# The end of a selective-scan block: six slots and a hand-ordered tail become one written list

## The chip, the cores and the metric

The kernel runs on one core of a Trainium2 chip. The metric is device microseconds of one execution, from start to end, and the time of a kernel is the median of several executions. Beside the times there is one profiled execution with a record of every instruction; its time and its span (first to last instruction) are told apart below. The core's engines run side by side, each in the order in which its instructions were written: TensorE (PE, with weight loads as PEld), VectorE (DVE), ScalarE (ACT), GpSimd (POOL) and SyncE (SP), which here only issues transfers.

## What is computed

For x of shape 4 x 128 x 96 x 96 the block adds to x a mixture of four scans of the normalised image (rows and columns, forward and backward). Cut to its core:

```
def _scan1d(x, ...):
    t = _grouped1x1(x, in_proj_w, in_proj_b, G)
    u, gate = t[:, :HID], t[:, HID:]
    u = depthwise_conv5(silu(u))
    s = _conv1x1(u, ssm_in_w)
    a = DMIN + (DMAX - DMIN) * sigmoid(_conv1x1(u, ssm_delta_w, ssm_delta_b))
    bb, cc = tanh(_conv1x1(u, ssm_b_w, ssm_b_b)), tanh(_conv1x1(u, ssm_c_w, ssm_c_b))
    h[l] = a[l] * h[l-1] + bb[l] * s[l]
    u = u + _conv1x1(cc * h + ssm_d * s, ssm_out_w)
    u = _grouped1x1(u * sigmoid(gate), mix_w, mix_b, G)
    return _conv1x1(u, out_proj_w, out_proj_b)
y = concat(scan of rows, rows reversed, columns, columns reversed)
x = x + einsum(fuse_w, y) + fuse_b
```

The reference writes the recurrence of h with cumulated logarithms; the line above is what it amounts to.

## The kernel before

Four images, for each a column pass (V) and a row pass (H), each pass six steps, each step four residues p in the order 1, 0, 3, 2: that makes NPAIR = 192 **pairs**, numbered n. A pair is two scans at once (s = 0 forward, s = 1 backward) over 384 positions. mix_w, out_proj_w and fuse_w are multiplied into one matrix w_fin beforehand, so a pair's last product goes straight to the 128 output channels and is added to `acc`, which holds the image's x in SBUF. The steps of the second half of a pass meet the positions of the first half again, so their silu values and gates come back from DRAM (`load_silu`, `load_kept`, `load_last`) and need no in-projection.

The work on a pair is cut into short **operations**, written by `emit` (L965). With engine, line and what each does:

- PE, L184: C0 C1 (convolution by bands), L (its rest, where p is not an edge), P1a P0a P1b P0b (projections to a, b, c, s), W00 W01 W10 W11 (result, s then half j). PE, L810: S00 S01 S10 S11 (state into the hidden channels).
- DVE: T1 to T4 (taps, L731), E (edge tap, L712, in place of L where p is 0 or 3), SCAN0 SCAN1 (L789, the two halves of a step's recurrence, once per four pairs), GAT0 GAT1 (times gate, L863).
- ACT: T0 (L729), UC (L694), TM (L747), SC (L755), CT (L758), SS (L776), UND0 UND1 (L806, copies u under the state), YS0 YS1 (L874, L876, takes the result out of its bank).
- POOL: DEC (L769), BS (L772), CH (L795), ADD (L799), CP (L803, copies the state's input to the other 64 partitions; on ACT for the last six pairs), ACC0 ACC1 (L910, adds the result to acc).

Within a pair the order of need is: C, L, T0 to T4; P; TM, SC, CT; DEC, BS; SCAN over four pairs; CH, ADD, CP; UND and S into the same banks; GAT; W; YS; ACC; and, for the second half of a row pass, the transfer of finished stretches of acc to `out` (`send`, L880).

**Order.** The engines run under a manual schedule: the order of writing is the order on each engine. `slot(t)` (L998) writes slot t by one of four texts in PLAN, picked by t modulo 24 (slots 186 and 187 use "none", 188 to 191 "front"). Each operation has a lag: slot t holds C of pair t, W of pair t - 7, and so on. After slot 191, `tail` (L1046) writes what is left by hand: for each of the last pairs S, then W of the pair before, GAT, UND of the next, CH ADD CP of the one after, and `finish` (L1036), which adds s = 0 on POOL from YS0 and s = 1 on DVE straight from the bank.

**Banks.** PSUM has eight banks, and twelve would be wanted: taps, convolution and the two UND/S/GAT groups take two each, P1a/P0a/TM, P1b/P0b/SC/CT and the two W groups one each. `rent` hands a bank to the first operation of a group, by the text's wish if that bank is free, else the one given back longest ago; `give` returns it after the group's last operation. A PE operation whose bank was read by DVE or ACT before waits for that reading.

**Loads.** SP issues in order. `load_edge` (L705) fills a tile with one buffer; `load_kept` fills one of two gate tiles for pair n + 2 after GAT of pair n; `load_last` brings the last four pairs' gates into a silu tile, after slot 189. A step's four transfers of 384 KB to `out` go after the step's last pair.

Of the kernel before, what the change touches and what calls it, by code (L numbers as in the profile page):

```python
# [47 lines left out]
P = 128  # L48
# [70 lines left out]
}  # L119
TBUFS, YBUFS, SEEDS = 6, 1, ()  # L120
ORDER = (1, 0, 3, 2)
# [4 lines left out]
def conv_preact_kernel(  # L126
# [769 lines left out]

    def accumulate(n, s, adder=nc.gpsimd):
        un = units[2 * n + s]
        p, st, y = un["p"], un["st"], yss.pop((n, s))
        if s == 1:  # L900
# [9 lines left out]
        adder.tensor_add(part, y, part)  # L910
        if un["order"] == "H" and un["st"] >= NS // 2 and un["k"] == R - 1:
            done[s].extend((un["b"], bass.ts(2 * st + e, LN * WW // 2)) for e in range(2))
# [68 lines left out]
    def release(kind):  # L981
        while held and loaded[pair_of(held[0][1])["b"]] == 2 * NS:
            emit(*held.pop(0), kind)

# [13 lines left out]
    def slot(t):  # L998
        now[0] = t
        kind = slot_kind(t)  # L1000
        for op in PLAN[kind].split():
            n = t - LAGS.get(op, 0)
            if op == "PIECE":
                if later and later[1] and t % R != 1:
                    free[:] = rent("tiny", kind)
                    later[1] = next(later[0], None)
# [12 lines left out]
            else:  # L1019
                if op == "YS0":  # L1020
                    load_next()
                if op[:2] == "YS":
                    if sum(h[0][3] == op[2] for h in held) == 2 - int(op[2]):
                        release(kind)
                emit(op, n, kind)
# [9 lines left out]

    def finish(n):  # L1036

        accumulate(n, 0)
        b = where.pop(("W1b", n))[0]
        yss[n, 1] = bank(b)[:, :N]  # L1040
        accumulate(n, 1, nc.vector)
        give([b])
        send(0)
        send(1)

    def tail():  # L1046

        def run(n, ops):
            for op in ops.split():
                if op == "DECV":  # L1050
                    decay(n, nc.vector)
                else:
                    emit(op, n, "none")

        last = NPAIR - 1
        run(last - 4, "CH")
        run(last, "P1b P0b")
        run(last - 7, "YS1")
        run(last - 6, "W00 W01 W10 W11")
        run(last - 4, "ADD")  # L1060
        run(last, "TM SC CT DECV BS")
        run(last - 5, "CP UND0 UND1 S00 S01 S10 S11")
        run(last - 3, "SCAN0 SCAN1")
        run(last - 7, "ACC1")
        run(last - 5, "GAT0 GAT1")
        run(last - 4, "CP")
        run(last, "SS")
        run(last - 1, "SS")
        run(last - 6, "YS0 YS1 ACC0")
        run(last - 4, "UND0 UND1")  # L1070
        run(last - 5, "W00 W01 W10 W11")
        run(last - 4, "S00 S01 S10 S11")
        run(last - 3, "CH ADD CP")
        run(last - 6, "ACC1")
        run(last - 5, "YS0")
        finish(last - 5)
        run(last - 4, "GAT0 GAT1")
        run(last - 3, "UND0 UND1")
        run(last - 2, "CH ADD CP")
        for n in range(last - 3, last + 1):  # L1080
            run(n, "S00 S01 S10 S11")
            run(n - 1, "W00 W01 W10 W11 YS0")
            run(n, "GAT0 GAT1")
            if n < last:
                run(n + 1, "UND0 UND1")
            if n + 2 <= last:
                run(n + 2, "CH ADD CP")
            finish(n - 1)
        run(last, "W00 W01 W10 W11 YS0")
        finish(last)  # L1090

# [24 lines left out]
    for op in PLAN["front"].split():  # L1116
        for n in range(-LAGS.get(op, 0)):
            if op[0] != "F" and op[:3] != "SIL":
                emit(op, n, "front")
    with tc.manual_schedule(  # L1120
# [3 lines left out]
    ):  # L1124
        for t in range(NPAIR):
            slot(t)
# [79 lines left out]
```

## Time and profile before

| what | us |
|---|---|
| median of 3 runs | 1815.69 (1810.68 to 1819.12) |
| profiled execution, its own time | 1816.33 |
| profiled execution, its span | 1814.6 |
| PE busy in it | 1761.8 (97%) |
| DVE busy | 1516.6 (84%) |
| ACT busy | 1492.9 (82%) |
| POOL busy | 1410.5 (78%) |

The profile's page gives busy time by engine, the span in 40 slices (a digit is a tenth), the granted TensorE clock, the chain of waits that ended last, and groups of instructions. The trace behind it can be asked for an engine's instructions in order of time (start, length, engine, line, operation, output <- input, shape, count, and in brackets the idle time before and what ended it), for busy times by stretches, and for transfers. PE rows count an f32 matmul twice, so C0 and C1 together, eight matmuls, are x16. A PE row's length includes the emptying of the array, so pitches are taken from start to start. The end of the program is where the core does worst: the last two of PE's 40 slices are the only ones below 9 after the second.

### The profile page before, as it was taken

What the parts mean: (1) busy time and instruction counts of PE and PEld (TensorE: products, weight loads), DVE (VectorE), ACT (ScalarE), POOL (GpSimd) and SP (SyncE); (2) the same over time, 40 slices, a digit from 0 to 9 for tenths busy, and PEclk for the clock granted to TensorE, in tenths of its full rate; (3) what the DMA queues carried; (4) which work ended last, traced back from release to release, by engine and by line L of the source; (5) the groups of instructions that cost most, each with busy time, mean ns of one, the idle gap of its engine ahead of it and who ended that gap; (6) DMA issues with size and microseconds to landing.
All of it is one profiled execution on the core that took longest, in us unless ns stands there. A gap on an engine that the chain in (4) does not pass through costs nothing.

```text
span 1814.6 us, 54530 instructions
## 1 busy us (share of the span) xinstructions
PE 1761.8 (97%) x22560; PEld 638.5 (35%) x22560; DVE 1516.6 (84%) x1538; ACT 1492.9 (82%) x2582; POOL 1410.5 (78%) x1504
## 2 busy tenths in 40 slices
PE   6899999999999999999999999999999999999987
PEld 3233333333333333333333333333333333333332
DVE  4788988888789988988888898888888888788874
ACT  4788888888888888888888888888888888888864
POOL 4478888778778888787777888877777888877884
PEclk7999999999999999999999999999999999999998
DMA  8467676665987578555897667656598765756452
GB/s 249 132 206 239 190 228 178 201 210 168 285 264 248 196 223 238 174 195 155 245 284 236 219 199 235 187 190 210 167 276 250 247 207 152 216 163 208 164 211 82
DMA packets 182568, 377.70 MB, mean 208 GB/s; under 512 B 16688, under 2 KB 145840, under 8 KB 182320
## 3 DMA queue, kind: packets, MB, share of 16 engines
q1 hardware_dynamic: 181888, 373.24, 66.2%
q8 instruction: 178, 2.92, 0.7%
q10 hardware_dynamic: 432, 0.96, 0.1%
q14 instruction: 70, 0.57, 0.1%
HBM read 222.96 MB, written 151.18 MB: 206 GB/s over the span
## 4 chain that ended last, share of the span: by engine, by line
PE 85%; DMA 4%; DVE 3%; ACT 3%; issue 2%; SPq 1%; POOL 1%; POOLq 0%; DVEq 0%; ACTq 0%
PE psum L184 72%; PE psum L810 9%; PE psum L816 4%; DMA acc<-in_xr 2%; DVE psum L731 1%; DMA out<-acc 1%; DMA edge<-edge 1%; ACT gate L822 1%; DVE u L863 1%; ACT psum L806 0%; POOL acc L910 0%; DVE u L731 0%; SPq L659 0%; ACT psum L729 0%; POOL t L772 0%
## 5 line engine op out<-in xcount | busy, mean ns | idle before, releaser
L731 DVE SCALAR_TENSOR_TENSOR psum<-sil,small,psum 128x768 f32<-128x768 f32 x576 | 588.6, 1022 | 55.2 <-ACT psum L729 37.0
L184 PE MATMUL psum<-u,w_fin 128*32 128x384 f32 x6144 | 585.9, 494 | 6.3 <-DVE u L863 3.0
L910 POOL TENSOR_TENSOR acc<-ys,acc 128x384 f32<-128x384 f32 x378 | 441.3, 1176 | 177.8 <-ACT ys L874 85.1
L184 PE MATMUL psum<-u,main 128*32 128x384 f32 x6144 | 563.9, 489 | 8.6 <-DVE u L712 3.3
L863 DVE SCALAR_TENSOR_TENSOR u<-gate,psum 128x768 f32<-128x768 f32 x376 | 345.8, 951 | 109.3 <-PE psum L810 81.0
L184 PEld LDWEIGHTS psum<-u,main 128*32 128x32 f32 x6144 | 185.5, 110 | 331.3 <-issue 213.8
L806 ACT COPY psum<-u 128x768 f32<-128x768 f32 x352 | 277.7, 801 | 29.4 <-DVE u L731 12.6
L184 PEld LDWEIGHTS psum<-u,w_fin 128*32 128x32 f32 x6144 | 176.0, 110 | 352.4 <-issue 247.0
L184 PE MATMUL psum<-sil,band 128*32 128x384 f32 x3072 | 284.9, 487 | 7.1 <-DVE u L731 2.7
L795 POOL TENSOR_TENSOR t<-t,t 64x384 f32<-64x384 f32 x192 | 235.0, 1224 | 62.2 <-DVE t L789 28.3
L810 PE MATMUL psum<-t,main 32*128 32x384 f32 x1536 | 263.6, 532 | 6.1 <-ACT psum L806 6.1
L799 POOL TENSOR_TENSOR t<-t,t 64x384 f32<-64x384 f32 x192 | 237.5, 1237 | 7.8
L822 ACT ACTIVATE gate<-psum,bnorm 128x384 f32<-128x384 f32 x384 | 212.4, 577 | 37.0 <-PE psum L810 16.4
L772 POOL TENSOR_TENSOR t<-t,tm 64x384 f32<-64x384 f32 x192 | 197.5, 1029 | 54.8 <-ACT t L755 46.7
L769 POOL TENSOR_SCALAR t<-tm 64x384 f32<-64x384 f32 x191 | 180.8, 947 | 74.5 <-ACT tm L747 35.8
L593 ACT ACTIVATE sil<-psum,bnorm 128x385 f32<-128x385 f32 x384 | 199.9, 582 | 26.8 <-PE psum L184 23.6
L731 DVE SCALAR_TENSOR_TENSOR u<-sil,small,psum 128x768 f32<-128x768 f32 x192 | 194.7, 1014 | 19.2 <-DVE psum L731 1.4
L729 ACT ACTIVATE psum<-sil,small 128x768 f32<-128x768 f32 x192 | 173.8, 905 | 33.4 <-DVE u L863 26.2
L816 PE MATMUL psum<-x_in,wn 32*128 32x384 f32 x768 | 188.5, 516 | 0.4 <-ACT gate L822 0.4
L747 ACT ACTIVATE tm<-psum,small 128x384 f32<-128x384 f32 x192 | 112.4, 585 | 66.9 <-PE psum L184 64.8
L184 PEld LDWEIGHTS psum<-sil,band 128*32 128x32 f32 x3072 | 97.4, 110 | 162.3 <-issue 104.6
L876 ACT COPY ys<-psum 128x384 f32<-128x384 f32 x282 | 135.1, 479 | 23.1 <-POOL acc L910 12.2
(83 smaller groups left out, 1440.7 us busy)
## 6 DMA issues: line engine op xcount, KB each, us to landing
sil<-sil SPq DMA_DIRECT2D x128, 770.0 KB, 6.8
kept<-gate SPq DMA_DIRECT2D x80, 768.0 KB, 4.5
gate<-kept SPq DMA_DIRECT2D x76, 768.0 KB, 6.1
edge<-edge SPq DMA_DIRECT2D x96, 384.0 KB, 6.6
x_in<-in_xs SPq DMA_DIRECT2D x192, 96.2 KB, 3.6
edge<-sil SPq DMA_DIRECT2D x96, 192.5 KB, 3.6
out<-acc SPq DMA_DIRECT2D x48, 384.0 KB, 3.7
acc<-in_xr SPq DMA_DIRECT2D x38, 384.0 KB, 8.4
```

What stands on the lines that cost most here:

```text
L184: nc.tensor.matmul(o[r, : rhs.shape[-1]], lhsT, rhs, start=start, stop=stop, skip_group_check=True)
L593: nc.scalar.activation(sils[step][:, s, j, g, :], bank(frm)[:, : N + 1], AF.Silu, bias=bn[:, 1:2] if j else bn[:, 4 + g : 5 + g],)
L731: nc.vector.scalar_tensor_tensor(u_of(n)[:, :, 1, :] if k == K - 1 else part, src, w_tap[:, k : k + 1], part, ALU.mult, ALU.add,)
L772: nc.gpsimd.tensor_mul(scan_of(n)[0:64, pair_of(n)["p"], :], tbs[n][0:64, :], tms[n][0:64, :])
L795: nc.gpsimd.tensor_mul(ta[0:64, p, :], tbs[n][64:P, :], ta[64:P, p, :])
L799: nc.gpsimd.tensor_add(z, scans[n // R][0:64, pair_of(n)["p"], :], z)
L806: nc.scalar.copy(two(to), us[n][:, s])
L810: nc.tensor.matmul(bank(to)[:, :N], w_so[r, bass.ts(j, P)], tbs[n][r, :], start=not seeded(n), stop=True, skip_group_check=True)
L816: nc.tensor.matmul(bank(to)[:, :N], stats[pair_of(n)["b"]][0][r, s, :], x_in[s][r, q, off : off + N], start=True, stop=True)
L822: nc.scalar.activation(gates[n % 2][:, s, j, :], bank(frm)[:, :N], AF.Tanh, bias=bn[:, 2 + j : 3 + j], scale=0.5,)
L863: nc.vector.scalar_tensor_tensor(v, g, 1.0, two(frm), ALU.add, ALU.mult)
L910: adder.tensor_add(part, y, part)
```

## The change

Slots 186 to 191 and the tail are dropped. In their place stands END, one list of operations for everything that is left, read from left to right: `T1:-6=2` is T1 of pair 192 - 6 = 186, and =2 is the bank wished for if it is the first operation of its group. Operations that do not apply (E of a pair that is no edge) are passed over, as `emit` did before.

Four operations with a star take another engine: CP* runs on ACT, DEC* on DVE, and ACC0*, ACC1* add on DVE straight from the bank (`add_bank`); the YS of the same pair is then left out, and for s = 0 the bias b_fin is added in the same instruction. 16 of the 27 adds in the list have the star, 3 of 7 DEC, 5 of 12 CP.

For the last four pairs (`final`) the sum of result and acc goes into the buffers x_in, idle by then, and each residue's 128 x 384 part is sent at once, two transfers of 192 KB per pair, in place of four of 384 KB behind the last pair. They lie in `out` in another order, which the host turns round by layout alone. `send` follows each ACC; `load_edge` follows an E, `load_kept` the second GAT of a pair, and `load_last` the last reader of the silu tile of pairs up to 187.

```diff
--- before.py
+++ after.py
@@ -117,6 +117,43 @@
+END = """
+    YS1:-14=3 C1:-6 TM:-7=7 CP*:-12 C0:-6=0 W00:-13 T1:-6=2 W01:-13=2 T2:-6 P0b:-7=0 P1b:-7=3
+    UND1:-12 E:-6 UND0:-12=1 ACC1:-14 T3:-6 S10:-12=4 T4:-6 S00:-12 YS0:-13=0 SC:-7 DEC:-7
+    S11:-12=5 S01:-12=0 GAT0:-12=2 T0:-5=5 W11:-13 ACC0:-13 T1:-5=2 W10:-13=0 CH:-11 BS:-7
+    ACC1*:-13 ADD:-11 C0:-5=6 CT:-7=6 GAT1:-12=6 P0a:-6=7 C1:-5 CH:-10 UND0:-11=0 CP:-11 T2:-5=7
+    P1a:-6=1 TM:-6=4 L:-5 W00:-12 CH:-9 T3:-5 P0b:-6=7 ADD:-9 W01:-12=5 S00:-11=6 UC:-5
+    UND1:-11=4 DEC:-6 T4:-5=6 S01:-11=7 ACC0*:-12 S11:-11 T0:-4=5 GAT0:-11 S10:-11=4 SS:-8
+    P0a:-5 P1a:-5=1 W11:-12=7 P1b:-6=4 W10:-12=7 TM:-5=1 T1:-4=3 P1b:-5=6 SC:-6 CT:-6=6 YS1:-12
+    ADD:-10 T2:-4 P0b:-5=2 T3:-4=2 C0:-4 W00:-11=6 SC:-5=5 GAT1:-11=6 DEC:-5 BS:-6 T4:-4=6
+    UND1:-10 BS:-5 W01:-11=3 C1:-4 YS1:-13=6 ACC1:-12 CP:-9 CP*:-10 SCAN0:-8 UND0:-10 S01:-10=2
+    S00:-10=3 S11:-10=0 S10:-10=2 L:-4=6 YS0:-11=7 ACC0:-11 CT:-5 W11:-11=2 GAT0:-10 T0:-3=7
+    GAT1:-10 W10:-11=5 W01:-10 UC:-4=2 W11:-10=1 W00:-10=6 W10:-10=2 T1:-3=5 T2:-3 T3:-3=1
+    ACC0*:-10 YS1:-11 ACC1:-11 YS1:-10=0 C0:-3=4 C1:-3=4 SS:-6 P1a:-4=4 P0a:-4 UND1:-9=1 SS:-7
+    P0b:-4 S11:-9=0 S10:-9 T4:-3=5 UND0:-9=6 ACC1:-10 SCAN1:-8 S01:-9=5 TM:-4 S00:-9=7 E:-3=1
+    P1b:-4=1 CH:-5 T0:-2 GAT1:-9 P1a:-3=3 CH:-8 P0a:-3 C1:-2=5 SS:-5 TM:-3=1 ADD:-8 C0:-2
+    GAT0:-9 T1:-2 UND0:-8 P1b:-3=5 E:-2 CP:-8 SC:-4=4 T2:-2=5 P0b:-3 CT:-4 W00:-9=2 W01:-9=5
+    T3:-2=5 UND1:-8=4 S01:-8 S10:-8 T4:-2=5 CT:-3=6 YS0:-9=7 BS:-4 YS0:-12=7 S00:-8=5 SC:-3=7
+    S11:-8=1 ADD:-5 ACC0:-9 DEC:-4 T0:-1=3 W10:-9 GAT1:-8 W11:-9=0 P1a:-2=1 P0a:-2 C1:-1
+    GAT0:-8=5 P0b:-2=0 C0:-1=6 T1:-1=5 P1b:-2 T2:-1 CH:-7 ADD:-7 W01:-8=4 W00:-8=1 YS1:-9=4
+    ACC1:-9 TM:-2=3 BS:-3 UND0:-7=6 SC:-2=4 T3:-1 L:-1 CP:-7 CH:-6 CT:-2=3 T4:-1=2 SS:-4 ADD:-6
+    P1a:-1=1 UND1:-7=0 S01:-7 S10:-7 S11:-7=7 ACC0*:-8 CP:-6 DEC*:-2 UC:-1=3 S00:-7 SS:-3
+    P0b:-1=4 DEC*:-3 YS0:-8 GAT1:-7=3 P0a:-1=7 UND0:-6=1 UND1:-6=4 P1b:-1=4 TM:-1=2 BS:-2
+    S10:-6=4 GAT0:-7=4 S11:-6 S01:-6 SC:-1=2 CP*:-5 S00:-6 W10:-8=5 CT:-1=4 W11:-8=2 BS:-1
+    UND1:-5=6 YS1:-8 W00:-7 ACC1:-8 DEC*:-1 GAT0:-6 UND0:-5=7 W01:-7=0 W01:-6 SCAN0:-4 W00:-6=5
+    YS0:-7=2 S10:-5 ACC0:-7 SS:-1 SS:-2 SCAN1:-4 CH:-4 S11:-5=3 GAT1:-6=3 S00:-5=5 S01:-5=2
+    ADD:-4 W11:-7 CH:-3 W10:-7=3 GAT0:-5 W10:-6=5 YS1:-7=5 CH:-2 UND1:-4=2 ACC0*:-6 W11:-6=7
+    ADD:-3 W01:-5=6 YS0:-6 YS0:-10 CP:-3 UND0:-4=1 GAT1:-5 W00:-5=6 CP*:-4 S00:-4 ACC1*:-6
+    S01:-4 ACC0*:-5 UND1:-3=7 S10:-4 ADD:-2 GAT0:-4 S11:-4=4 W11:-5=2 YS0:-5 GAT1:-4=5 W10:-5=4
+    W01:-4=3 UND0:-3=1 W00:-4=2 ACC1*:-5 CH:-1 CP*:-2 YS0:-4=0 S11:-3=5 S00:-3=0 ACC0*:-4
+    S01:-3=0 S10:-3=1 GAT0:-3=6 W10:-4=1 W11:-4=1 GAT1:-3 W01:-3 W00:-3=4 UND0:-2=4 UND1:-2
+    ACC1*:-4 ACC0*:-3 S11:-2 ADD:-1 S01:-2=5 S00:-2=1 UND0:-1 ACC1:-7 S10:-2=5 GAT0:-2=3
+    W11:-3=7 CP:-1 W10:-3=2 UND1:-1 GAT1:-2=2 W00:-2=6 S11:-1=3 ACC1*:-3 S01:-1 S00:-1=3 S10:-1
+    YS1:-6 YS1:-4=0 W01:-2=5 YS0:-3=1 YS1:-3 W10:-2 W11:-2 GAT0:-1=2 W00:-1 ACC0*:-2 W01:-1=0
+    YS1:-2=6 GAT1:-1=4 ACC1*:-2 YS0:-2=7 W11:-1=0 ACC0*:-1 W10:-1=0 YS1:-5=6 YS0:-1 ACC1*:-1
+    YS1:-1=0
+"""
+TAIL = 6
...
-    def rent(ten, kind):
+    def rent(ten, want):
         wide = ten in ("TB", "CB", "SS0", "SS1")
-        want = BANKS[kind].get(ten)
...
     def copy_z(n):
-        copy = nc.scalar.copy if n >= NPAIR - 6 else nc.gpsimd.tensor_copy
-        copy(tbs[n][64:P, :], tbs[n][0:64, :])
+        nc.gpsimd.tensor_copy(tbs[n][64:P, :], tbs[n][0:64, :])
+    def copy_z_scalar(n):
+        nc.scalar.copy(tbs[n][64:P, :], tbs[n][0:64, :])
...
-    def accumulate(n, s, adder=nc.gpsimd):
+    added = [0, 0]
+    def accumulate(n, s, frm=None):
         un = units[2 * n + s]
-        p, st, y = un["p"], un["st"], yss.pop((n, s))
+        p, st = un["p"], un["st"]
+        y = yss.pop((n, s)) if frm is None else bank(frm)[:, :N]
         if s == 1:
             y, p, st = y[:, ::-1], R - 1 - p, NS - 1 - st
         if un["order"] == "V":
@@ -907,8 +948,20 @@
         else:
             part = acc[:, bass.ts(st, LN), p, :]
             y = y.rearrange("p (h m) -> p h m", m=M)
-        adder.tensor_add(part, y, part)
-        if un["order"] == "H" and un["st"] >= NS // 2 and un["k"] == R - 1:
+        final = n >= NPAIR - R
+        to = x_in[s][:, p, :N].rearrange("p (h m) -> p h m", m=M) if final else part
+        if frm is None:
+            nc.gpsimd.tensor_add(to, y, part)
+        elif s == 0:
+            nc.vector.scalar_tensor_tensor(to, y, b_fin, part, ALU.add, ALU.add)
+        else:
+            nc.vector.tensor_add(to, y, part)
+        if final:
+            nc.sync.dma_start(out[un["b"], :, bass.ts(R * st + p, N)], x_in[s][:, p, :N])
+        elif un["order"] == "H" and un["st"] >= NS // 2:
+            added[s] += 1
+            if added[s] % R:
+                return
             done[s].extend((un["b"], bass.ts(2 * st + e, LN * WW // 2)) for e in range(2))
...
-    def emit(op, n, kind):
+    def emit(op, n, wants):
         if not active(op, n):
             return
+        if op[-1] == "*":
+            return OTHERS[op](n)
         if op not in rents:
             return FUNCS[op](n)
         ten, which = rents[op]
         if (ten, n) not in where:
-            where[ten, n] = rent(ten, kind)
+            where[ten, n] = rent(ten, wants.get(ten))
             left[ten, n] = sum(active(q, n) for q in TENANTS[ten])
...
-        if t == NPAIR - 3:
-            load_last()
...
-    def finish(n):
-        accumulate(n, 0)
-        b = where.pop(("W1b", n))[0]
-        yss[n, 1] = bank(b)[:, :N]
-        accumulate(n, 1, nc.vector)
-        give([b])
-        send(0)
-        send(1)
+    def add_bank(n, s):
+        del left[f"W{s}b", n]
+        banks = where.pop((f"W{s}b", n))
+        accumulate(n, s, banks[0])
+        give(banks)
+    OTHERS = {
+        "CP*": copy_z_scalar,
+        "DEC*": lambda n: decay(n, nc.vector),
+        "ACC0*": lambda n: add_bank(n, 0),
+        "ACC1*": lambda n: add_bank(n, 1),
+    }
     def tail():
-        def run(n, ops):
...
-        run(last, "W00 W01 W10 W11 YS0")
-        finish(last)
+        items = [x.partition("=") for x in END.split()]
+        items = [(*op.split(":"), int(b) if b else None) for op, _, b in items]
+        readers = sum(
+            op[0] in "CTL" and op[1:] in "01234" and NPAIR + int(n) < NPAIR - R for op, n, _ in items
+        )
+        taken = {(op[3], n) for op, n, _ in items if op in ("ACC0*", "ACC1*")}
+        gating_of, due = {}, [n for n in range(NPAIR - TAIL + 1, NPAIR) if edged(n)]
+        for op, m, want in items:
+            n = NPAIR + int(m)
+            if op[:2] == "YS" and (op[2], m) in taken:
+                continue
+            emit(op, n, {rents[op][0]: want} if op in rents else {})
+            if op in ("GAT0", "GAT1"):
+                gating_of[n] = gating_of.get(n, 0) + 1
+                if gating_of[n] == 2:
+                    load_kept(n + 2)
+            elif op == "E" and due:
+                load_edge(due.pop(0))
+            elif op[:3] == "ACC":
+                send(int(op[3]))
+            if op[0] in "CTL" and op[1:] in "01234" and n < NPAIR - R:
+                readers -= 1
+                if not readers:
+                    load_last()
...
-        for t in range(NPAIR):
+        for t in range(NPAIR - TAIL):
             slot(t)
         tail()
...
-    y = r.results[0]["out_0"].reshape(B, DIM, HH, R, M)
+    y = np.array(r.results[0]["out_0"]).reshape(B, DIM, NS, LN * WW)
+    for st in (0, NS - 1):
+        last = y[-1, :, st].reshape(DIM, R, LN, M)
+        y[-1, :, st] = last.transpose(0, 2, 1, 3).reshape(DIM, LN * WW)
+    y = y.reshape(B, DIM, HH, R, M)
     return np.ascontiguousarray(y.transpose(0, 1, 2, 4, 3)).reshape(B, DIM, HH, WW)
```

More of the change, by code (lines that the diff above doesn't have):

```diff
@@ L982, in release @@
         while held and loaded[pair_of(held[0][1])["b"]] == 2 * NS:
-            emit(*held.pop(0), kind)
+            emit(*held.pop(0), BANKS[kind])
     MOVE = {
@@ L1004, in slot @@
                 if later and later[1] and t % R != 1:
-                    free[:] = rent("tiny", kind)
+                    free[:] = rent("tiny", BANKS[kind].get("tiny"))
                     later[1] = next(later[0], None)
@@ L1024, in slot @@
                         release(kind)
-                emit(op, n, kind)
+                emit(op, n, BANKS[kind])
         for move in MOVES[kind].split():
             MOVE[move](t)
-        if t == NPAIR - 3:
-            load_last()
         if 2 * R <= t < NPAIR:
@@ L1034, in slot @@
                 free.clear()
-    def finish(n):
-        accumulate(n, 0)
-        b = where.pop(("W1b", n))[0]
-        yss[n, 1] = bank(b)[:, :N]
-        accumulate(n, 1, nc.vector)
-        give([b])
-        send(0)
-        send(1)
-    def tail():
-        def run(n, ops):
[L1049 to L1088, printed above, removed]
-        run(last, "W00 W01 W10 W11 YS0")
-        finish(last)
@@ L1118, in conv_preact_kernel @@
             if op[0] != "F" and op[:3] != "SIL":
-                emit(op, n, "front")
+                emit(op, n, BANKS["front"])
     with tc.manual_schedule(
```

## The prediction

> **What bounds the kernel now.** I read the page first: the span, the busy slices, the granted clock.
>
> ```profile
> span 1814.6 us, 54530 instructions
> PE   6899999999999999999999999999999999999987
> PEclk7999999999999999999999999999999999999998
> ```
>
> PE is full in every slice but the first two and the last two, so PE sets the pace and the change, which touches only the end, can win only what the end loses. The busy times by stage show how much that is. The first stage begins where PE starts slot 186 (the band matmuls of pair 186, at 1715.07), which is where the written list takes over.
>
> ```profile
> 1715.00:1734.50 19.50, 18.67 (x228) 6.60 (x220) 16.29 (x17) 14.96 (x24) 17.67 (x19) 1.00 0.28 96
> 1734.50:1769.00 34.50, 30.53 (x368) 10.75 (x372) 24.96 (x25) 20.85 (x34) 27.86 (x27) 1.00 0.64 226
> 1769.00:1787.00 18.00, 12.95 (x96) 4.06 (x88) 10.69 (x9) 10.25 (x17) 13.29 (x12) 0.76 0.09 37
> 1787.00:1808.30 21.30, 19.98 (x186) 6.80 (x184) 9.20 (x13) 8.20 (x13) 7.41 (x7) 0.88 0.19 75
> 1808.30:1814.60 6.30, 0.00 (x0) 0.00 (x0) 0.00 (x0) 0.00 (x0) 0.00 (x0) 0.83 0.63 250
> ```
>
> Columns: length, busy PE, PEld, DVE, ACT, POOL, clock, DMA share, GB/s. PE loses 0.8 us of the first stage, 4.0 of the second and 5.0 of the third; in the third and fourth its clock is down as well; in the last, 6.3 us, only a DMA runs. Now the order of PE's work in the third and fourth stage.
>
> ```profile
> 1776.49 5.35 PE L184 MATMUL psum<-u,w_fin 128*32 128x384 f32 x32 [3.02 <-DVE u L863]
> 1784.72 2.42 PE L810 MATMUL psum<-t,main 32*128 32x384 f32 x8 [2.03 <-ACT psum L806]
> 1787.08 5.21 PE L184 MATMUL psum<-u,w_fin 128*32 128x384 f32 x32
> 1802.13 5.37 PE L184 MATMUL psum<-u,w_fin 128*32 128x384 f32 x64
> 1778.00:1780.00 2.00, 2.00 (x16) 0.50 0.00 0
> ```
>
> After a wait of 3.02 us (for GAT, which stood behind both scans on DVE) and one of 2.03 us, 32 result matmuls take 5.35 and 5.21 us; the last row has 64 in 5.37, so 32 take 2.7 at full speed. The window row (length, PE, clock, DMA share, GB/s) says why: the granted clock was 0.50. That is 2.6 + 2.5 = 5.1 us lost to the clock.
>
> **The change, part by part.** *PE's work* is the same matmuls in another order. The rows give the pitch of each kind, from the start of one row to the start of the next.
>
> ```profile
> 1715.07 1.47 PE L184 MATMUL psum<-sil,band 128*32 128x384 f32 x16
> 1716.36 0.83 PE L184 MATMUL psum<-u,main 128*32 128x384 f32 x8
> 1719.06 0.93 PE L810 MATMUL psum<-t,main 32*128 32x384 f32 x8
> 1719.91 0.85 PE L184 MATMUL psum<-u,main 128*32 128x384 f32 x8
> 1724.57 0.88 PE L184 MATMUL psum<-sil,less 64*32 64x384 f32 x16
> 1725.37 0.85 PE L184 MATMUL psum<-u,w_fin 128*32 128x384 f32 x8
> 1738.95 2.76 PE L184 MATMUL psum<-u,main 128*32 128x384 f32 x32
> 1741.53 1.47 PE L184 MATMUL psum<-u,w_fin 128*32 128x384 f32 x16
> ```
>
> C0 and C1 together 1.29 us, so 0.645 each; four S items 0.85, so 0.21 each; L 0.80; x32 in 2.58, so 0.645 for each P or W item (8 rows). The list has 12 C, 26 P and 52 W items (90 x 0.645 = 58.05), 48 S (10.2) and 3 L (2.4): 70.65 us. From 1715.07 that ends at 1785.7, against the 1807.5 at which the row of 1802.13 ends now: 21.8 us is the most that order can win on PE.
>
> *DVE's work* grows: 16 adds read the bank directly (6 do so now), three DEC are there instead of one.
>
> ```profile
> 1705.97 3.14 DVE L731 SCALAR_TENSOR_TENSOR psum<-sil,small,psum 128x768 f32<-128x768 f32 x3
> 1709.21 1.01 DVE L731 SCALAR_TENSOR_TENSOR u<-sil,small,psum 128x768 f32<-128x768 f32 x1
> 1710.14 1.01 DVE L712 SCALAR_TENSOR_TENSOR u<-edge,small,psum 128x768 f32<-128x768 f32 x1
> 1711.18 1.81 DVE L789 TENSOR_TENSOR_SCAN t<-t 64x768 f32<-64x768 f32 x1
> 1713.03 1.82 DVE L863 SCALAR_TENSOR_TENSOR u<-gate,psum 128x768 f32<-128x768 f32 x2
> 1714.76 2.08 DVE L731 SCALAR_TENSOR_TENSOR psum<-sil,small,psum 128x768 f32<-128x768 f32 x2
> 1768.86 1.32 DVE L769 TENSOR_SCALAR t<-tm 64x384 f32<-64x384 f32 x1 [2.33 <-ACT tm L747]
> 1771.06 2.54 DVE L789 TENSOR_TENSOR_SCAN t<-t,t 64x768 f32<-64x768 f32 x1 [0.88 <-POOL t L772]
> 1773.63 1.81 DVE L789 TENSOR_TENSOR_SCAN t<-t 64x768 f32<-64x768 f32 x1
> 1781.90 0.56 DVE L910 TENSOR_TENSOR acc<-psum,acc 128x384 f32<-128x384 f32 x1 [4.61 <-PE psum L184]
> ```
>
> Four taps take 4.17 (1705.97 to 1710.14), E 1.04, SCAN1 1.85, GAT 0.865 (two in 1.73), SCAN0 2.57, DEC 1.32, an add 0.56. DVE starts T1 of pair 186 at 1714.76. In the list up to SCAN1 of pair 188 stand 6 x 4.17 + 3 x 1.04 + 13 x 0.865 + 4 x 0.56 + 3 x 1.32 + 2 x (2.57 + 1.85) = 54.4 us, so that scan ends at 1769.2 (1775.4 now); behind it 11 GAT and 12 adds, 16.2 us. DVE's sum, 70.6, equals PE's. The add with b_fin (s = 0) is a SCALAR_TENSOR_TENSOR, which no row shows with 384 elements: between 0.56 (the add) and 0.95 (GAT, twice the elements); I take 0.56, since the form costs no more per element in GAT than in the add, and keep 9 x 0.39 = 3.5 us for the range.
>
> *ACT and POOL* have room. All 77 ACT items at the longest one's time make 69.7 us, all 51 POOL items likewise 63.1; both overstate.
>
> ```profile
> L729 ACT ACTIVATE psum<-sil,small 128x768 f32<-128x768 f32 x192 | 173.8, 905 | 33.4 <-DVE u L863 26.2
> L799 POOL TENSOR_TENSOR t<-t,t 64x384 f32<-64x384 f32 x192 | 237.5, 1237 | 7.8
> ```
>
> So the 16 YS that leave ACT and the adds that leave POOL are worth nothing of themselves; they shorten chains. CP on ACT (5 of 12) hides in ACT's slack; without it the next S would wait 0.5 us.
>
> *The end behind the scan.* POOL's CH and ADD of pair 188 (2 x 1.24) and CP on ACT (0.5, with hand-overs 0.7) put its S at 1769.2 + 3.2 = 1772.4. From there PE has 16 S and 18 W items, 15.0 us: 1787.4. The last add brings 1788.0. The other path, POOL to CP of pair 191 (four CH, four ADD, two CP, one ACC, about 12.8 us) and then S, GAT, W and add (4.5), ends at 1786.5. Laying each engine's items end to end by these pitches and comparing each PE item's start with the end of the DVE item that it needs (GAT for W, T4 for P, the last reader for a bank), none comes more than 1.9 us too early (W10 of pair 186, behind the scans), and no DVE item comes more than 0.9 us ahead of its W. So the list leaves hardly a gap, and no cushion either.
>
> What waits cost is the unknown. Below: nothing, 1788.0. Above: the second stage's density, 88.5% (30.53 of 34.5), which puts PE's end at 1715.07 + 70.65/0.885 = 1794.9. I take the first stage's loss, 0.83 of 19.5 or 4.3%, since there too the order was mixed pair by pair: 3.0 us. One wait comes on top, of a load.
>
> *The way out.* Now POOL ends the last add at 1808.28, four transfers of 384 KB are issued, and the span ends 6.3 us later.
>
> ```profile
> 1807.29 0.99 POOL L910 TENSOR_TENSOR acc<-ys,acc 128x384 f32<-128x384 f32 x1 [1.87 <-ACT ys L874]
> 1808.31 2.32 SPq L882 DMA_DIRECT2D out<-acc  x4
> DMA  0000100000000000000000005999999999800000
> ```
>
> The DMA line has slices of 0.375 us from 1800: data flow from 1809.0 (0.7 after the first issue) to 1813.1, and the span ends 1.5 later. 1.5 MB in 4.1 us is 375 KB per us, so the 192 KB of the last residue take 0.5: 0.7 + 0.5 + 1.5 and 0.1 hand-over, 2.8 us. The other seven transfers are issued behind earlier adds; four issues more than now, 0.58 us each on SP (2.32 for four), which has nothing else to send by then. Bounds: 2.8 and 6.3.
>
> *Loads moved.* The edge tile has one buffer. The list loads it for pair 189 behind E of 186, long ahead, but for pair 190 behind E of 189, and between the two E stand only two GAT and T1, 2.8 us.
>
> ```profile
> edge<-edge SPq DMA_DIRECT2D x2, 384.0 KB, 4.6
> edge<-edge SPq DMA_DIRECT2D x96, 384.0 KB, 6.6
> gate<-kept SPq DMA_DIRECT2D x3, 768.0 KB, 4.2
> 1749.92 3.98 SPq L851 DMA_DIRECT2D last_gates<-kept x4
> ```
>
> The first and third rows are medians from issue to landing between 1700 and 1740, the second is that of the whole run. DVE, with everything behind E, waits 1.8 us by the first and 3.8 by the second; nothing if something else makes T1 late. Nothing else is being loaded by then, so I take the low side: 1.2 us. The gate load of pair 187 starts behind GAT of 185 and has 7.3 us, enough at 4.2. The four last_gates loads go ahead once T4 of pair 187 is out (1726 by the DVE sum), long before GAT of 188. Out transfers of earlier steps wait on SP for their adds, but no load that is due stands behind them.
>
> **Sum.** Last add 1788.0 + 3.0 + 1.2 = 1792.2, span 1792.2 + 2.8 = 1795.0 (1814.6 now). The profiled execution's own time was 1816.33, 1.7 above its span, so 1796.7; it was 0.6 above the median 1815.69. Prediction 1796.
>
> **Rivals.** (1) *The list stalls as stage two does*: PE's end 1794.9, add 0.6, way out 2.8, plus 1.1: 1799.4, with the b_fin adds dear 1803. For it: DVE and PE have equal sums and eight banks serve twelve users. Against it: the item check above.
>
> (2) *The clock falls in the last stage.* One wait of 3 us costs itself and 5 to 7 us at clock 0.50, as at 1776: 1805.5; if the 15.0 us behind the scan ran wholly at 0.50, 1811. For it: PE's items there wait for DVE again and again. Against it: in stage two waits of 0.9 to 2.1 us stand at clock 1.00.
>
> The Trainium skill ("TensorE: Matmul & The Clock Gate", "HAM oscillation — how this bites in real kernels", with its second failure mode) speaks against the change here: short PE waits between groups while PSUM banks are cycled can make the clock swing, not only a gap over about 3.4 us. By that rule rival 2 holds, 1805 to 1811; stage two does not bear it out.
>
> (3) *Slower: the adds block DVE.* DVE works in order, so an add that waits for W holds the taps and GATs behind it, and PE waits for those.
>
> ```profile
>   PE psum L184: 14.7, 6
> ```
>
> The six DVE adds of now waited 14.7 us, 2.45 each. Were that the price of all 16, DVE would end at 1714.8 + 70.6 + 39.2 = 1824.6, and 2.8 + 1.1 make the time 1828.5. It decides (over 1824.8) from 2.2 us per add. Against it: the old adds wait where DVE has nothing else to do, while by the sums the list's first add (pair 179) is reached at 1721.9 and its W is out at 1721.1.
>
> **How the numbers follow.** Forecast 0.60, rival 1 0.25, rival 2 0.10, rival 3 0.05. The forecast alone spans 1790 (no waits and PE's own end at 1785.7, with add, way out and the 1.1) to 1800. Half of rival 2 stays under 1806.6, the 0.5% (9.1 us) that a measurement of this kernel can tell; so faster 0.60 + 0.25 + 0.04, no change 0.06, slower 0.05. The runs of now spread over 8 us, so I widen the range at the lower end to 1788, and take in rival 1 and the cheap half of rival 2: to 1806.
>
> **What would show it.** The second scan of pair 188 ending near 1769 to 1771; PE over 95% busy from 1715 to its end at clock 1.00; about 20 us from that scan to the last add; under 3.2 us from there to the end; DVE over 93% busy. A PE wait over 2.5 us, a clock of 0.50 behind 1769, or DVE idle before the adds would prove rivals 1 to 3.

## The result and the profile after

Four executions of the changed kernel took 1792.2 to 1795.76 us, median **1793.44**; the kernel before took a median of 1816.22 in four beside them. The ratio is 0.988, 95% interval 0.9853 to 0.9906. Between the medians that is 22.8 us, where 19.7 (to 1796) were forecast; in the last group of runs below it is 18.5. The profiled execution has a span of 1794.0 us against 1814.6, so 20.6 of it can be read in the traces.

The page of the changed kernel: span, PE's busy slices, granted clock.

```profile
span 1794.0 us, 54508 instructions
PE   6899999999999999999999999999999999999998
PEclk7999999999999999999999999999999999999999
```

The two weak slices at the end (8 and 7) have become 9 and 8, and the clock's last slice, 8 before, is 9: its dips are gone. Busy times by stage (length, PE, PEld, DVE, ACT, POOL, clock, DMA share, GB/s):

```profile
1715.00:1734.50 19.50, 19.37 (x240) 6.77 (x232) 17.57 (x20) 13.82 (x23) 17.48 (x18) 1.00 0.56 190
1734.50:1769.00 34.50, 33.24 (x396) 12.10 (x397) 32.58 (x32) 25.50 (x43) 24.74 (x24) 1.00 0.56 192
1769.00:1788.00 19.00, 18.84 (x208) 6.65 (x212) 15.96 (x22) 8.04 (x12) 13.65 (x12) 1.00 0.33 126
1788.00:1794.00 6.00, 2.21 (x28) 0.65 (x20) 1.64 (x3) 0.00 (x0) 0.00 (x0) 1.00 0.36 132
```

In the second stage DVE is busy 32.6 us of 34.5 (25.0 before) and PE 33.2 (30.5): here the two run side by side near their limits, as the two equal sums said. In the third stage PE is still full (18.84 of 19.0) but DVE is not (15.96, 84%). From 1769 to the last add it was 39.3 us before, and is 21.8 now.

Profiles differ in the time that the program needs up to pair 186: this kernel begins it at 1714.42 here and at 1717.79 in a second profile, the kernel before at 1715.07. So I measure the **tail**: from the start of the first convolution of pair 186 to the end of the span. Before, it lasted 99.5 us. The rows that mark it now, in order of time on PE and DVE:

```profile
1714.42 1.47 PE L221 MATMUL psum<-sil,band 128*32 128x384 f32 x16
1767.85 2.38 DVE L825 TENSOR_TENSOR_SCAN t<-t 64x768 f32<-64x768 f32 x1
1785.49 4.72 PE L221 MATMUL psum<-u,w_fin 128*32 128x384 f32 x56
1790.27 0.56 DVE L958 TENSOR_TENSOR x_in<-psum,acc 128x384 f32<-128x384 f32 x1 [0.67 <-PE psum L221]
```

| from 186's first C to | before | forecast (from 1715.07) | after |
|---|---|---|---|
| end of pair 188's second scan | 60.4 | 54.1, waits apart | 55.8 |
| end of PE's last matmul | 92.4 | 76.5 | 75.8 |
| end of the last add | 93.2 | 77.1 | 76.4 |
| end of the span (tail) | 99.5 | 79.9 | 79.6 |

PE has 70.65 us of work in the tail and finishes in 75.8. The longest of its waits, and where DVE waited, by the rows and the waits of 1715 to 1794 (total, times, longest):

```profile
1764.02 0.93 PE L848 MATMUL psum<-t,main 32*128 32x384 f32 x8 [0.97 <-ACT psum L844]
1759.28 2.78 DVE L805 TENSOR_SCALAR t<-tm 64x384 f32<-64x384 f32 x2
1748.77 1.02 DVE L748 SCALAR_TENSOR_TENSOR u<-edge,small,psum 128x768 f32<-128x768 f32 x1 [0.68 <-DMA edge<-edge]
DVE x_in L956 <- PE psum L221: 1.4, 3, 0.5
DVE acc L956 <- PE psum L221: 0.7, 2, 0.5
DVE x_in L958 <- PE psum L221: 0.7, 1, 0.7
```

PE's wait of 0.97 is for UND1 of pair 186, whose bank GAT1 of pair 185 had still to read; GAT1 stood behind two DEC on DVE (the second row). E of pair 190 waited for its edge rows, as foreseen. And 16 adds together waited 2.8 us, where six had waited 14.7. Up to the second scan of pair 188 DVE waited 2.9 us in all, behind it 4.2, there nearly always for PE.

### The profile page after: what moved, and what is told of

It is laid out like the page before. It is cut to its first block, busy times and chain, and to the rows that moved or that the text cites. A ratio compares the mean times of both kernels' runs of the same rounds, so it can differ in the third digit from the quotient of the medians.

```text
span 1794.0 us, 54508 instructions
## 1 busy us (share of the span) xinstructions
PE 1754.7 (98%) x22560; PEld 637.5 (36%) x22560; DVE 1523.2 (85%) x1550; ACT 1485.4 (83%) x2571; POOL 1401.1 (78%) x1493
## 4 chain that ended last, share of the span: by engine, by line
PE 88%; ACT 3%; DMA 3%; DVE 2%; issue 2%; POOL 2%; SPq 1%; POOLq 0%; ACTq 0%; DVEq 0%
PE psum L221 74%; PE psum L848 9%; PE psum L854 4%; DMA acc<-in_xr 1%; DMA out<-acc 1%; ACT gate L860 1%; POOL acc L954 1%; ACT psum L844 1%; DVE bn L372 0%; DVE psum L767 0%; ACT sil L629 0%; DVE u L901 0%; POOL t L831 0%; POOL t L808 0%; SPq L695 0%
## 5 line engine op out<-in xcount | busy, mean ns | idle before, releaser
L221 PE MATMUL psum<-u,w_fin 128*32 128x384 f32 x6144 | 580.0, 490 | 2.0 <-DVE u L748 0.7
L954 POOL TENSOR_TENSOR acc<-ys,acc 128x384 f32<-128x384 f32 x368 | 431.4, 1181 | 160.9 <-ACT ys L914 79.7
L767 DVE SCALAR_TENSOR_TENSOR u<-sil,small,psum 128x768 f32<-128x768 f32 x192 | 194.7, 1014 | 18.8 <-DVE psum L767 1.4
L765 ACT ACTIVATE psum<-sil,small 128x768 f32<-128x768 f32 x192 | 173.9, 906 | 34.5 <-DVE u L901 27.6
```

What stands on the lines that cost most here:

```text
L221: nc.tensor.matmul(o[r, : rhs.shape[-1]], lhsT, rhs, start=start, stop=stop, skip_group_check=True)
L767: nc.vector.scalar_tensor_tensor(u_of(n)[:, :, 1, :] if k == K - 1 else part, src, w_tap[:, k : k + 1], part, ALU.mult, ALU.add,)
L954: nc.gpsimd.tensor_add(to, y, part)
```

## The experiments

Twelve runs: eleven kernels with one or two things undone, added or moved, and the change once more. Tails are from one profiled execution each, times are medians, with the ratio to runs of the kernel before beside them. Two profiles of the changed kernel agree in their tails to 0.1 us (79.6, 79.7). Groups of runs differ by some microseconds: the changed kernel, run again with the last group, took 1798.5, and its ratio was 0.9899 (0.9876 to 0.9922). The times expected below were often missed (e1, e3, e9, e11, e13 and e14 by 0.4 to 5.6 us, all upward), that of the change itself among them; the expectations are judged by the tail.

| kernel | tail | last add after 186's first C | way out | median us | ratio to before (95%) |
|---|---|---|---|---|---|
| before | 99.5 | 93.2 | 6.3 | 1816.22 | 1 |
| old order, waits filled (e11) | 94.4 | 88.2 | 6.2 | 1811.68 | 0.9973 (0.9961 to 0.9985) |
| list alone (e9) | 88.4 | 82.2 | 6.2 | 1803.38 | 0.994 (0.992 to 0.996) |
| list, results by residue (e3) | 85.2 | 82.0 | 3.2 | 1801.54 | 0.9931 (0.9909 to 0.9952) |
| list, direct adds (e13) | 82.1 | 76.5 | 5.6 | 1798.9 | 0.9905 (0.9882 to 0.9928) |
| the change | 79.6 | 76.4 | 3.2 | 1793.44 | 0.988 (0.9853 to 0.9906) |
| the change again (e14) | 79.7 | 76.4 | 3.3 | 1798.5 | 0.9899 (0.9876 to 0.9922) |

### The three parts taken apart

**The way out.** Sums into acc, four transfers of 384 KB behind the last pair:

```diff
-        final = n >= NPAIR - R
+        final = False
```

> The written list with its direct adds, but the last step's sums go into acc and leave as four transfers of 384 KB behind the last pair, as before. From the start of pair 186's first convolution to the end of the span took 99.5 us before and 79.6 us with the change (the tail). Theory: the way out is worth what the two spans show behind the last add, 6.3 - 3.2 = 3.1 us, and nothing else depends on it: tail 82.7, time 1796.5. Rival: the earlier small transfers only move the same waiting for memory, tail below 80.5.

Tail 82.1, way out 5.6 us, median 1802.06, ratio 0.9925 (0.9899 to 0.9951). In this kernel, and in e9 below, the adds of the last two steps are counted together, so one stretch of `out` goes out twice and another not at all; number and size of the transfers are as meant. With the counts apart:

```diff
-            added[s] += 1
-            if added[s] % R:
+            x = s + 2 * (n >= NPAIR - R)
+            added[x] += 1
+            if added[x] % R:
```

> The list with its direct adds, the last step's sums into acc and out in four transfers of 384 KB behind the last pair, now with the adds of the last two steps counted apart so that each stretch goes out once and when it is complete. Theory: way out 6.3 in place of 3.2 us, all else as with the change: tail 82.7, time 1796.5. Rival: below 80.5.

The same tail, 82.1, and all else stands still (last add at 76.5 against 76.4). The way out is worth 2.5 us here, a little under the 3.1 expected: in the list s = 0 is added 1.3 us before s = 1, so two of the four transfers start before the last add, and 5.6 remain of 6.3.

The same part alone, in the old order:

```diff
-        adder.tensor_add(part, y, part)
+        adder.tensor_add(to, y, part)
+        if final:
+            nc.sync.dma_start(out[un["b"], :, bass.ts(R * st + p, N)], x_in[s][:, p, :N])
```

> The order of before, but the last four pairs' sums go into the x_in buffers and leave by residue, 192 KB each. Theory: worth 3.1 us by itself, tail 96.4 (99.5 before), time 1813. Rival: the way out is worth more in the old order since three of the four pairs' data also leave early and the chip's memory is quiet at the end, tail below 95; or it is worth nothing without the list, tail 99.

Way out 3.3 us as expected, 3.0 saved; but the tail was 93.2 and not 96.4, because PE's last matmul, which the edit does not touch, ended 3.3 us earlier. The rows of e2 (PE in order of time, then windows: length, PE, clock, DMA share, GB/s) show why:

```profile
1775.59 2.79 PE L184 MATMUL psum<-u,w_fin 128*32 128x384 f32 x32 [3.03 <-DVE u L863]
1781.26 1.69 PE L810 MATMUL psum<-t,main 32*128 32x384 f32 x8 [2.02 <-ACT psum L806]
1782.88 2.79 PE L184 MATMUL psum<-u,w_fin 128*32 128x384 f32 x32
1776.00:1778.00 2.00, 2.00 (x32) 1.00 0.01 4
```

The same two waits as before, 3.03 and 2.02 us, and this time the clock stayed at 1.00 behind them: 32 matmuls take 2.79 in both places, where the profile of before has 5.35 and 5.21. So the loss to the clock at these two waits does not come in every execution. The ten executions of e2 fall into two groups: three at 1807.3 to 1808.3 us with a mean clock of 0.992, seven at 1811.8 to 1814.7 with 0.989 to 0.991. Of the 13 of before in that group of runs, two had 0.992 (1808.6 and 1812.6), eleven 0.986 to 0.990 (1814.0 to 1820.8). Over all executions the ratio of e2 is 0.998 (0.9965 to 0.9995), which agrees with the 3 us of the way out.

This profile lost its clock at another place, at a wait that the profile of before passed at full clock (1745.11 there, 2.11 us, then 1.50 for the same 16 matmuls):

```profile
1742.69 2.66 PE L184 MATMUL psum<-sil,band 128*32 128x384 f32 x16 [2.11 <-ACT ys L874]
```

From 1744 to 1746 the granted clock was 0.50. So e2 gained 4.8 us at the two later waits and lost 1.5 here, which makes the 3.3.

**The direct adds.** All s = 0 adds and the one of pair 179 go back to YS and POOL, at the same places in the list (the six s = 1 adds that DVE did before stay):

```diff
-    ... ACC0*:-12 ...
+    ... YS0:-12 ACC0:-12 ...
```

> The list with the adds shared as before: all s = 0 adds and the one of pair 179 go through YS on ACT and an add on POOL (ten more YS, ten more POOL adds, ten fewer DVE adds), at the same places of the list; x_in and the sending by residue stay. Theory: four of these adds then stand before CP of pair 191 on POOL, 4 x 1.08 us in the chain behind the second scan, and the last add ends later: tail 84 to 86, time 1798 to 1800. Rival 3 of the prediction (adds that wait on DVE hold up taps and GATs): DVE is freed, the tail gets shorter than 79.6, time below 1793.

Tail 85.2, inside the theory's 84 to 86: 5.6 us longer. POOL and PE of e3, in order of time:

```profile
1785.16 1.01 POOL L952 TENSOR_TENSOR x_in<-ys,acc 128x384 f32<-128x384 f32 x1 [0.79 <-ACT ys L910]
1786.13 1.22 POOL L833 TENSOR_TENSOR t<-t,t 64x384 f32<-64x384 f32 x1
1787.32 1.00 POOL L952 TENSOR_TENSOR acc<-ys,acc 128x384 f32<-128x384 f32 x1
1788.38 0.50 POOL L836 COPY t<-t 64x384 f32<-64x384 f32 x1
1788.93 0.93 PE L846 MATMUL psum<-t,main 32*128 32x384 f32 x8 [1.30 <-POOL t L836]
```

CP of pair 191 ends at 1788.88, 17.8 us after the scan's end, where it took 13.1 in the changed kernel (1770.23 to 1783.32), and PE's S of pair 191 waits 1.30 us for it. That is the theory's chain, but not all of it: the second scan of pair 188 already ends 2.2 us later here (58.0 us after 186's first C, 55.8 in the changed kernel), and 3.4 us are lost behind it. Where the 2.2 come from was not taken apart. Rival 3, adds that hold up DVE, is refuted for this list: with fewer adds on DVE both the scan and the end come later.

**The list alone**, with neither of the two:

> The list's order and banks alone: adds shared between POOL and DVE as before, sums into acc, four transfers at the end. Theory: order alone is worth a little over half of the 20 us of the trace, and the other two parts add to it: tail 87 to 89, time 1801 to 1803. Rival: the order is the whole gain apart from the way out, tail 83; or the order needs the direct adds and alone wins under 5 us, tail above 94.

Tail 88.4, inside 87 to 89. So the list is worth 11.1 us of tail, the direct adds 6.3 more (88.4 to 82.1, of which 0.6 are transfers that start earlier), the residues 2.5: 19.9 in all. The 11.1 hold, beside the order, the DEC and CP that the list puts on other engines and the loads that it moves; no run takes these apart.

### What the list's 11.1 us are made of

The prediction put 5.1 us of the old tail down to the clock. To test it without the list, PE's two waits were filled with matmuls that nobody reads; `fill(4)` writes four of them into the free bank that was given back longest ago. A first try:

```diff
         run(last - 4, "UND0 UND1")
+        fill(4)
         run(last - 5, "W00 W01 W10 W11")
...
+        fill(3)
         for n in range(last - 3, last + 1):
```

> The order of before with seven matmuls of 0.65 us each whose results nobody reads, four in PE's wait of 3.0 us and three in that of 2.0 us, into a bank that is free there. Nothing else is touched, so PE's waits are filled and the rest starts when it did. Theory: the two waits let the granted clock fall in most executions of before (clock 0.986 to 0.990 and 1814 to 1821 us in eleven of thirteen, 0.992 and 1809 to 1813 in two); with the waits filled the clock stays at 1.00 in all of them, mean 0.992, and the time falls by about 5 us to 1809 to 1811. Rival: the fall has another cause, or the seven matmuls hold the work up by as much: no change within 2 us, mean clock below 0.991.

Tail 101.5, 1814.2 us, ratio 1.0003 (0.9993 to 1.0014): no gain, but only the second, shorter wait was filled. The row shows that the first `fill` got a bank that GAT had still to read, so the four matmuls waited as W had, and then ran slowly (5.49 us where the next try has 2.85):

```profile
1773.41 5.49 PE L1058 MATMUL psum<-u,w_fin 128*128 128x384 f32 x8 [3.03 <-DVE u L863]
```

Written right behind the S before each wait, into a bank free since long:

```diff
         run(last - 5, "CP UND0 UND1 S00 S01 S10 S11")
+        fill(4)
...
         run(last - 4, "S00 S01 S10 S11")
+        fill(3)
```

> The order of before with the seven unread matmuls again, now written straight behind S of pair 186 (four) and S of pair 187 (three), into a bank that has been free for long, so that they wait for nothing and run inside PE's waits of 3.0 and 2.0 us. Theory: the clock stays at 1.00, the two times 32 result matmuls take 2.8 us each in every execution, tail 94 to 95 (99.5 in the profile of before), times 1808 to 1811 throughout with a mean clock of 0.992. Rival: the fall of the clock is not tied to these waits, or the matmuls hold up S and W: tail over 98, times spread as before.

PE rows of e11, and the window that was at 0.50 before:

```profile
1773.84 2.85 PE L1058 MATMUL psum<-u,w_fin 128*128 128x384 f32 x8
1776.94 2.79 PE L184 MATMUL psum<-u,w_fin 128*32 128x384 f32 x32 [0.25 <-DVE u L863]
1780.52 2.20 PE L1058 MATMUL psum<-u,w_fin 128*128 128x384 f32 x6
1784.23 2.79 PE L184 MATMUL psum<-u,w_fin 128*32 128x384 f32 x32
1778.00:1780.00 2.00, 2.00 (x28) 1.00 0.03 8
```

The work that the program needs starts no sooner than before, only PE is no longer idle there, and the tail is 94.4 (94 to 95 expected). One profile at full clock could be chance, as e2 shows; the other executions decide. The 12 took 1808.5 to 1814.9 us (1808 to 1811 expected), median 1811.68, with a mean clock of 0.990 to 0.992; 14 of the 17 of before beside them had 0.987 to 0.990. The ratio, 0.9973 (0.9961 to 0.9985), clears 1. So the clock's share of a profile like that of before is 5.1 us. The remaining 6.0 of the list's 11.1 are, by subtraction, waits of PE that the list closes: by the traces PE waited 10.5 us in the tail of before and 4.9 in that of e9.

### Banks, loads and the list's cushion

**Bank wishes** away, so each group takes the bank given back longest ago:

```diff
-    YS1:-14=3 C1:-6 TM:-7=7 ...
+    YS1:-14 C1:-6 TM:-7 ...
```

> The changed kernel without the bank numbers in the list, so each group takes the bank given back longest ago. Theory: PE and DVE stand within 1 to 2 us of each other all along, so a bank whose reader is late costs at once: tail 83 to 92 (79.6 with the wishes), time 1797 to 1805. Rival: the oldest bank is as good as the chosen one, tail within 1 us of 79.6, and the order of the list is all.

Tail 80.4, 1794.05 us, ratio 0.9898 (0.988 to 0.9916): the theory fails and the rival holds. The wishes are worth at most 0.8 us in the trace and nothing that the times could show. The gain does not rest on the banks.

**The edge of pair 190**, first loaded ahead into an idle buffer, then loaded later:

```diff
+        if n == NPAIR - 2:
+            t = edges[n] = x_in[0][:, 2:4, :N]
```

> The changed kernel, but the edge rows of pair 190 are loaded into the idle x_in buffer behind E of pair 186, long before they are needed; the 0.68 us that E of 190 waited for them goes. Theory (DVE has no cushion): tail 78.9 to 79.2. Rival (PE was late anyhow and takes the wait up): 79.6 within 0.2.

```diff
-            elif op == "E" and due:
+            elif op == "E" and len(due) == 2:
...
                     load_kept(n + 2)
+                    if n == NPAIR - 9:
+                        load_edge(due.pop(0))
```

> The changed kernel with the edge load of pair 190 issued behind GAT0 of pair 183 in place of behind E of pair 189, 1.8 us later: DVE's wait for it should grow from 0.7 to 2.4 us. Theory (no cushion): tail 81.0 to 81.4, PE waits by as much. Rival: DVE catches up before the second scan, tail below 80.2.

E of pair 190 on DVE, in e5 and in e6:

```profile
1748.78 1.01 DVE L751 SCALAR_TENSOR_TENSOR u<-x_in,small,psum 128x768 f32<-128x768 f32 x1
```

```profile
1750.06 1.02 DVE L748 SCALAR_TENSOR_TENSOR u<-edge,small,psum 128x768 f32<-128x768 f32 x1 [4.67 <-DMA edge<-edge]
1751.97 1.55 PE L848 MATMUL psum<-t,main 32*128 32x384 f32 x6 [3.20 <-ACT psum L844]
1753.45 2.50 PE L221 MATMUL psum<-u,w_fin 128*32 128x384 f32 x16
```

Ahead: no wait, tail 79.1, 0.5 shorter (the time, 1792.64, cannot tell). Late: the wait grew to 4.67 us and not to 2.4. The load was issued 2.1 us later and took 5.2 us to E in place of 3.3; it now stood behind the 768 KB gate load of pair 185 on SP, which is the likely reason and was not tested apart. The tail grew to 84.4, 4.8 us for 4.0 of added wait, and the time to 1797.3, ratio 0.9922 (0.9902 to 0.9943). Nothing in the list makes up for a wait on DVE there. More than the wait comes back: PE in turn waited 3.20 us, and the clock fell behind it (0.50 from 1753 to 1755; the third row has 2.50 us where x16 takes 1.50).

**Both mends together**: the edge ahead, and GAT1 of pair 185 written before the two DEC, to take away PE's longest wait. Two bank wishes change with it.

```diff
-    ... ACC0*:-8 CP:-6 DEC*:-2 UC:-1=3 S00:-7 SS:-3
-    P0b:-1=4 DEC*:-3 YS0:-8 GAT1:-7=3 P0a:-1=7 UND0:-6=1 UND1:-6=4 ...
+    ... ACC0*:-8 CP:-6 GAT1:-7=3 DEC*:-2 UC:-1=3 S00:-7 SS:-3
+    P0b:-1=4 DEC*:-3 YS0:-8 P0a:-1=7 UND0:-6=6 UND1:-6=2 ...
```

> The changed kernel with the edge of pair 190 loaded ahead (0.5 us of tail) and GAT1 of pair 185 written before the two DEC on DVE, so that UND1 of pair 186 and PE's S behind it no longer wait for 2.8 us of DEC (PE's longest wait, 0.97 us). Theory: the PE wait falls below 0.3, tail 78.1 to 78.5, time 1.0 to 1.5 us under the change's. Rival: the wait only moves to the next W or to the second scan, since DVE is full there: tail 79.0 or more.

```profile
1765.35 0.95 DVE L904 SCALAR_TENSOR_TENSOR u<-gate,psum 128x768 f32<-128x768 f32 x1 [1.87 <-ACT t L815]
1767.29 0.93 PE L851 MATMUL psum<-t,main 32*128 32x384 f32 x8
1776.40 2.79 PE L221 MATMUL psum<-u,w_fin 128*32 128x384 f32 x32 [1.36 <-DVE u L904]
```

The rival: PE's S no longer waits (second row), but GAT1 itself waits 1.87 us where DEC would have run (first row), the scan ends 56.2 us after 186's first C in place of 55.3 (e5), and W of pair 186 waits 1.36 (third row). Tail 80.0, 1799.41 us beside 1798.5 for the change, ratio 0.9902 (0.9881 to 0.9924). No run was clearly faster than the change.

The change again, as the measure for that group of runs:

> The changed kernel once more, beside the others on the same chip. Both theories: tail 79.6 within 0.5, time 1793.4 within 2, no execution with a mean clock under 0.991, since PE never waits over 1 us.

Tail 79.7; the five executions took 1795.5 to 1800.5 us with a mean clock of 0.991 to 0.993. The time missed its 1793.4 by 5.1 us, though the kernel before lay only 0.8 higher in that group than in the first; the two ratios, 0.988 and 0.9899, overlap. Of the 3.5 us by which the two profiles' spans differ, 3.4 lie ahead of pair 186, where the change does nothing. So times are compared by the ratio, ends by the tail.

## Why the prediction was right

*PE's end is the loss, 21.8 us at most.* Right: of the span's 20.6 us, 19.9 came from the tail. The other 0.65 is an earlier start of pair 186, which varies from profile to profile.

*Equal sums of PE and DVE, no cushion.* Right up to the second scan, and shown there: e6 passes its whole added wait on, e3 gains nothing from a freer DVE. Behind the scan it is PE alone that sets the pace. DVE was to be busy over 93%; it was busy 67.75 us of the 75.8 from 1715 to the last add, 89%, and the sign failed mostly by the waits behind the scan. By its rows DVE's items cost what was assumed, but for four: the add with b_fin takes 0.61 to 0.62, near the bound taken; two DEC took 1.39 each and the third 0.51 (1.32 taken); of the last step's scans SCAN0 took 1.81 (2.57) and SCAN1 2.38 (1.85). The last SCAN0, then the group of the b_fin adds into acc with count, busy and mean ns:

```profile
1765.99 1.81 DVE L825 TENSOR_TENSOR_SCAN t<-t,t 64x768 f32<-64x768 f32 x1
L956 DVE SCALAR_TENSOR_TENSOR acc<-psum,b_fin,acc 128x384 f32<-128x384 f32 x5 | 3.1, 614 | 0.7 <-PE psum L221 0.7
```

*The scan's end.* Forecast 1769.2 before waits, came at 1770.23 from a start 0.65 earlier: 1.7 us late. DVE's waits up to there are 2.9 us, and its items took 1.2 less than summed. The edge wait is 0.68 of the waits (1.2 forecast), which e5 confirms with 0.5 of tail.

*Behind the scan, 18.8 us and a share of the waits.* It took 20.6. Part of the difference has a row on POOL of the changed kernel:

```profile
1767.34 3.69 POOL L954 TENSOR_TENSOR acc<-ys,acc 128x384 f32<-128x384 f32 x2 [1.50 <-ACT ys L914]
1771.11 1.22 POOL L831 TENSOR_TENSOR t<-t,t 64x384 f32<-64x384 f32 x1
```

Two adds, which take 1.0 each in the rows of before where no scan runs, took 3.69 here, most of it beside the second scan, so CH of pair 188 began 0.88 us after the scan's end, and the chain of CH, ADD and CP started late. The prediction had POOL free at that point.

*Waits, 4.2 us in all.* Right in size: PE stood 5.1 us above its work; the forecast had 5.9, the 4.2 and the 1.7 that the chain behind the scan already puts on PE's end. The kind was left open: 3.0 of the 4.2 is a rate carried over from the first stage. By the rows only 1.25 of the 5.1 are marked waits (0.97 and 0.28). The rest is in pitches a little longer than summed, most of them at a change between kinds of matmul: 0.11 us from 1717.00 to 1718.40 (1.40 for x16, which makes 1.29), 0.36 from 1769.75 to 1773.98 (4.23 for x48, 3.87). The tail came within 0.3 us of the forecast in part by luck: the last add was 0.7 us earlier than summed, the way out 0.4 longer.

*"the 16 YS that leave ACT and the adds that leave POOL are worth nothing of themselves; they shorten chains".* Right in kind but never sized. It is 5.6 us by e3, more than a quarter of the gain. My sum held it without saying so, since POOL's 12.8 us behind the scan counted one add only (13.1 measured, 17.8 with the adds of e3).

*The way out, 2.8 us.* It took 3.2; by rows of the changed kernel:

```profile
1790.27 0.56 DVE L958 TENSOR_TENSOR x_in<-psum,acc 128x384 f32<-128x384 f32 x1 [0.67 <-PE psum L221]
DMA  0000006808999999593000194029209505900000
out<-x_in SPq DMA_DIRECT2D x7, 192.0 KB, 1.9
```

The slices of 0.35 us from 1780 show the last data until about 1792.3, 1.4 us behind the add, and the span ends 1.7 after that.

*The clock.* 5.1 us was right for the profiled execution, as e11 shows; wrong in that it was taken for granted in every execution. Some pass the two waits at full clock, as the profile of e2 did. The prediction's route to the median, 0.6 under the profiled execution, therefore carried a mixture that it did not know of.

*The rivals.* (1) PE's density over the tail was 70.65 of 75.8, 93%, not 88.5%. (2) The clock did not fall: 1.00 in all four stages. Where PE did wait 3.20 us in this list (e6), it fell; so the rival's mechanism exists, and the shorter waits of the changed kernel did not set it off. The prediction's argument against it, waits of up to 2.1 us at full clock in stage two, rested on one profile: in e2 and in e7 the clock fell to 0.50 behind the same wait of 2.11 us. The Trainium skill's second failure mode ("TensorE: Matmul & The Clock Gate", "A second HAM failure mode: psum-queue depth-cycling") did not show with waits of up to 0.97 us between groups. (3) 2.8 us of waiting for 16 adds, 0.17 each, against the 2.2 from which it would decide.

## What to carry to other kernels

At a pipeline's end, add up each engine's remaining work by pitches from the trace; the largest sum from the engine's present position, plus the shortest chain out, says what an order can reach, and comparing producers and consumers item by item says whether the written order reaches it. An operation moved to another engine is priced by the chain that it leaves, not by the busy time that it frees: ten adds taken from engines with room were worth 5.6 us. And if an engine has no idle time left, a load that has 2.8 us to land is on the path.

## What the runs showed of the hardware that was not expected

Whether the granted clock falls after a PE wait of 2 to 3 us differs from one execution to the next, with the same waits to 0.01 us. The same three waits in four profiles of the old order, with the clock behind each:

| profile | 2.11 us | 3.0 us | 2.0 us |
|---|---|---|---|
| before | 1.00 | 0.50 | 0.50 |
| e2 | 0.50 | 1.00 | 1.00 |
| e7 | 0.50 | 0.50 | filled |
| e11 | 1.00 | filled | filled |

In the list's profiles waits of up to 1.36 us (e12) left it at 1.00, and the one of 3.20 us (e6) did not. The times of e2 fall into two groups some 5 us apart (mean clock 0.992, and 0.989 to 0.991), those of before are spread, and a single profile shows one case.

The Trainium skill says as much of the start of a kernel ("TensorE: Matmul & The Clock Gate", "Part 1: The HAM clock gate (the "warmup" mystery)"): the activity window runs freely, so the same kernel meets it at another phase each time. The runs here agree in that the same wait ends differently, and show it in the middle of a kernel; a window was not measured.

Some operations of DVE and POOL are slower side by side: two POOL adds took 3.69 us, most of it beside a DVE scan (2.38, 1.81 with POOL mostly idle), and two DEC on DVE took 2.78 while POOL ran CH, ADD and CP, where the third, with POOL idle but for its last 0.1 us, took 0.51:

```profile
1764.42 0.51 DVE L805 TENSOR_SCALAR t<-tm 64x384 f32<-64x384 f32 x1 [0.52 <-ACT tm L783]
1764.83 1.02 POOL L808 TENSOR_TENSOR t<-t,tm 64x384 f32<-64x384 f32 x1 [1.32 <-ACT t L791]
```

A tap on DVE (1757.70, 1.01 us) beside BS on POOL (1757.50, 1.02) took its usual time. The reason was not looked for.
